# Half-row h.h score matmuls for two heads at once, and context products two slot blocks at a time

## The chip, the cores and the metric

The kernel runs on one core of a Trainium2 chip. Its engines are TensorE (PE: matmuls, with PEld for the loading of the stationary operand), VectorE (DVE), ScalarE (ACT), GpSimd (POOL) and SyncE (SP, which issues DMAs). The metric is the device time of one execution in microseconds (us). Three executions were timed: median 1238.76 us, from 1238.45 to 1245.84. The execution that the profiler recorded took 1251.64 us.

## The reference

Self-attention over 16 batches of 1024 tokens with width 512, with 8 heads of 64, in which the queries are keys and values too, added to the input:

```
q      = x^T Wq^T                     # per batch: 1024 x 512, seen as 8 heads of 64
scores = 0.125 * q q^T                # per head
logits = (scores * cmask + (1 - cmask) * -1e30) * rmask
ctx    = softmax(logits) q
out    = x + (ctx Wo^T)^T
```

The mask is 0 or 1 with about even odds. A masked row has equal logits, so its context is the mean of all q. An unmasked row needs only the unmasked tokens. The kernel therefore gathers the unmasked tokens of a batch into at most 544 slots and computes the attention among these.

## The kernel before, in words

**Precision.** q is split into two f16 parts, q = h + l. The scores of a head need h.h + h.l + l.h. `qsplit` (L388) makes a tile `hl` for each pair of heads (head 0 of the pair in rows 0 to 63, head 1 in rows 64 to 127; h first, l second), and copies it by six DMAs into a tile `xx`, in which each head has all 128 rows, once as h over l and once as l over h. For head k of the pair, xx[:, 2k] is the first and xx[:, 2k+1] the second.

**Scores.** `scores` (L497) makes, for one head and one block of 128 slots (i = 0 to 3), a 128 x 544 tile in PSUM, in two halves of 272 columns (g), each in a bank of its own. The stationary operand is h over l. Two matmuls over all 128 rows add up in each half: with h over l again (h.h + l.l) and with l over h (h.l + l.h). That makes four matmuls for each head and block (L530), 2048 in all. Then ScalarE takes the exponential into an SBUF tile `p` (L533), with the row sums. The score buffers (`pss`) are two, of two banks each. The tail of 32 slots (512 to 543) of four heads at a time is made in `scores(b, p, None)` (L510 to L524), in columns of 32.

**Context.** `attend` (L538) multiplies `p` of the two heads of a pair with the values, in f32: per block two halves of columns for each of two heads, four products (L546), each writing 64 of the 128 PSUM rows (head 0 the lower, head 1 the upper). The tail (i = 4, L549) closes the sum, and ScalarE copies the only context buffer `pav` out (L553).

**Order.** `run` (L724) goes batch by batch over 18 steps S: for each of four pairs the blocks 0 to 3, and two tail steps put in at places 2 and 11. In each step it issues the scores of both heads, and fills with a share of a list m: transposes (`xt`), queries (`query`, L380), values and the rest of the next batch, and the projection of the last one (L625). The share goes by the costs that stand in the list. `todo` holds the context products of the last block (the `attend` of one step is issued in the next), before or after the fill as `big` says. `whole` and `tail` carry the closing product of a pair into the next pair's first steps, between its two heads' scores. `free` holds, by step, work without a place in the list: `recip` two steps after a pair ends and `norm` four. What the loops issue is then put in order, engine by engine, by the framework's scheduler, which has costs of its own and follows the dependencies and the buffers; TensorE runs that order as it stands.

Of the kernel before, what the change touches and what calls it, by code (L numbers as in the profile page):

```python
# [10 lines left out]
F32 = mybir.dt.float32  # L11
F32R = mybir.dt.float32r
F16 = mybir.dt.float16
I32 = mybir.dt.int32
AF = mybir.ActivationFunctionType
# [4 lines left out]
P = 128  # L20
# [3 lines left out]
DK = 64  # L24
# [3 lines left out]
SCALE = 0.125  # L28
NEG = -1.0e30

C = 544
CT = C - 512
CH = C // 2
CQ = C + 2
CM = C
HG = H // 2
# [13 lines left out]
class Fast:  # L50
# [242 lines left out]
            s["xt"] = self.rows(s["idx"][:CT, 4:5], self.sb([P, D], F32, "xt"))  # L293

    def start(self, b):
        s = self.st[b] = {"xa": [], "xx": [], "v": [], "c": [], "nm": [], "corr": [], "rd": [], "xm": []}
        s["ms2"] = self.sb([P, 2 * DC], F32, "ms2", 2)

    def load_half(self, b, k, after=None):
# [88 lines left out]
    def qsplit(self, b, e):  # L388


        nc, s = self.nc, self.st[b]
        q = s["q"][:, e, :C]
        hl = self.sb([P, 2, C], F16, "hl", 1)
        nc.vector.tensor_copy(hl[:, 0, :], q)
        nc.vector.tensor_tensor(hl[:, 1, :], q, hl[:, 0, :], ALU.subtract)
        xx = self.sb([P, 4, C], F16, "xx", 5)
        lo, up = slice(0, DK), slice(DK, P)
        nc.sync.dma_start(out=xx[lo, 0:2, :], in_=hl[lo, :, :])
        nc.sync.dma_start(out=xx[up, 0, :], in_=hl[lo, 1, :])
        nc.sync.dma_start(out=xx[up, 1, :], in_=hl[lo, 0, :])  # L400
        nc.sync.dma_start(out=xx[lo, 2:4, :], in_=hl[up, :, :])
        nc.sync.dma_start(out=xx[up, 2, :], in_=hl[up, 1, :])
        nc.sync.dma_start(out=xx[up, 3, :], in_=hl[up, 0, :])
        s["xx"].append(xx)
# [92 lines left out]
    def scores(self, b, p, i):  # L497


        nc, s = self.nc, self.st[b]  # L500
        if "z" not in s:
            s["z"] = self.sb([P, H, 4], F32, "z", 2)
            s["zt"] = self.sb([P, 2], F32, "zt", 2)
        if i is None:
            pt = self.ps_s.tile([P, 2, 512], F32, tag="s", name="pss")
            for a in range(2):
                for g in range(2):
                    for r in range(HG):
                        xx, k = s["xx"][2 * p + r // 2], r % 2
                        nc.tensor.matmul(pt[r * CT:(r + 1) * CT, g, :CH], lhsT=xx[:, 2 * k, 512:C],  # L510
                                         rhs=xx[:, 2 * k + a, g * CH:(g + 1) * CH], start=(a == 0), stop=(a == 1))
            t = self.sb([P, C], F32, "p", 5)
            nc.scalar.activation(t.rearrange("p (g c) -> p g c", g=2), pt[:, :, :CH], AF.Exp,  # L513
                                 bias=s["nm"][p][:, HG:], scale=SCALE, accum_out=s["zt"][:, p:p + 1])

            hi = self.sb([P, C], F32R, "c", 3)
            lo = t.bitcast(F32R)
            nc.vector.tensor_copy(hi, t)
            nc.vector.tensor_tensor(lo, t, hi.bitcast(F32), ALU.subtract)
            s["pt"] = self.sb([P, 2, C], F32R, "pt")  # L520
            half = slice(0, DK), slice(DK, P)
            for k in range(2):
                nc.sync.dma_start(out=s["pt"][half[k], k, :].bitcast(F32), in_=hi[half[k]].bitcast(F32))
                nc.sync.dma_start(out=s["pt"][half[1 - k], k, :].bitcast(F32), in_=lo[half[k]].bitcast(F32))  # L524
            return None
        xx, k = s["xx"][p // 2], p % 2
        pt = self.ps_s.tile([P, 2, 512], F32, tag="s", name="pss")
        for a in range(2):
            for g in range(2):
                nc.tensor.matmul(pt[:, g, :CH], lhsT=xx[:, 2 * k, i * P:(i + 1) * P],  # L530
                                 rhs=xx[:, 2 * k + a, g * CH:(g + 1) * CH], start=(a == 0), stop=(a == 1))
        t = self.sb([P, C], F32, "p", 5)
        self.exp = [nc.scalar.activation(t.rearrange("p (g c) -> p g c", g=2), pt[:, :, :CH], AF.Exp,  # L533
                                         bias=s["nm"][p // HG][:, p % HG:p % HG + 1], scale=SCALE,
                                         accum_out=s["z"][:, p, i:i + 1]).ins]
        return t

    def attend(self, b, p, i, ps):  # L538
        nc, s = self.nc, self.st[b]
# [184 lines left out]
    def run(self, flag):  # L724
        B = self.B
        L = lambda f, *a: lambda: f(*a)
        S = [(p, i) for p in range(NP) for i in range(4)]
        S.insert(2, (0, None))
        S.insert(11, (1, None))
        N = len(S)  # L730

        def xt(n):
# [16 lines left out]
        for i, e in enumerate(ends):  # L749
            g = list(range(ends[i - 1] + 1 if i else 0, e + 1))  # L750
# [50 lines left out]
        begin += [(0, L(self.load, "o", c)) for c in range(DC)]  # L801
        begin += [(0, L(self.range_x, 0, c)) for c in range(DC)] + [(0, L(self.range_w, "q"))]
        groups = [(g, min(h, B)) for g, h in ((2, 4), (4, 8), (8, 12), (12, 16)) if g < B]
        todo, whole, tail = [], [], []
        for b in range(B + 1):
            o, n = b - 1, b + 1
            if b == B:
# [2 lines left out]
            free, early, late = {}, [], []  # L810
# [67 lines left out]
            for st, (p, i) in enumerate(S):  # L878
                for f in free.get(st, []):
                    f()  # L880
                if i is None:
                    self.scores(b, p, None)
                else:
                    ps = [self.scores(b, 2 * p, i)]
                    if tail:
                        tail.pop()()
                    ps.append(self.scores(b, 2 * p + 1, i))
                goal = total * (st + 1) / N
                fill = []
                while pos < len(m) and (done + m[pos][0] / 2 <= goal or st == N - 1):  # L890
                    fill.append(m[pos])
                    done += m[pos][0]
                    pos += 1

                big = st >= 4 and [c >= 1 for c, _ in fill if c > 0.1][:1] == [True]
                fill = [f for _, f in fill]
                now = [] if i is None else todo
                for f in fill + now if big else now + fill:
                    f()
                if i is not None:  # L900
                    todo = [L(self.attend, b, p, i, ps)]
                if whole and i == 0:
                    tail.append(whole.pop())
                if i == 3:
                    (whole if p < 3 else todo).append(L(self.attend, b, p, 4, None))
                    if p < 3:
                        free.setdefault(st + 2, []).append(L(self.recip, b, p))
                        free.setdefault(st + 4, []).append(L(self.norm, b, p))
            self.st.pop(b - 4, None)
        bad = self.const.tile([1, 1], F32, name="bad")  # L910
        self.nc.vector.tensor_reduce(bad, self.ok[0:1, :], AX.X, ALU.add)
# [145 lines left out]
```

## Time and profile before

| | |
|---|---|
| median of three executions | 1238.76 us |
| profiled execution, its own time | 1251.64 us |
| its span | 1249.9 us |
| TensorE matmuls busy | 1140.9 us (91%) |
| VectorE busy | 714.8 us (57%) |
| ScalarE busy | 693.6 us (55%) |
| GpSimd busy | 296.0 us (24%) |
| mean granted TensorE clock | 0.966 |
| context products L546, busy | 328.7 us in 2048 records |
| score matmuls L530, busy | 309.7 us in 2048 records |

In a line of a group stand the source line, the engine, the operation, the tiles written and read, the shapes and the count; then the busy time in us and the mean in ns of one, and the idle time of the engine just before them with what ended most of it. In "128*64 128x272" the first figures are the rows and columns of the array that are in use, the second the moving operand. The ends of matmuls are modelled and overlap with the next starts, so what one costs is read from start to start. In a timeline a row is: start in us, length in us, engine, line, operation, tiles, shape and count of what was merged into it.

### The profile page before, as it was taken

Reading aid. Unit: us, or ns where it says so; the run is one execution under the profiler, and the core shown is the slowest. Engines: PE = TensorE matmul, PEld = TensorE weight load, DVE = VectorE, ACT = ScalarE, POOL = GpSimd, SP = SyncE. Lnnn points to the kernel's source line nnn. Section 1 sums busy time; section 2 is a strip of 40 time slices with the busy share of each in tenths; the row PEclk is TensorE's granted clock in tenths of the full one; section 3 lists DMA queues with packets and bytes.
Section 4 is the critical chain, followed back from the end, with each engine's and each line's share of the span. In section 5 each row is a group of like instructions: output and inputs, shape, how many; then the busy total and the mean of one; then the engine's idle time right before and its main releaser. Section 6 shows DMA issues by size and latency. Waiting matters only on the chain. (4 is left out here: it accounts for less than half of the span.)

```text
span 1249.9 us, 23817 instructions
## 1 busy us (share of the span) xinstructions
PE 1140.9 (91%) x8354; PEld 694.5 (56%) x8354; DVE 714.8 (57%) x2262; ACT 693.6 (55%) x1828; POOL 296.0 (24%) x299
## 2 busy tenths in 40 slices
PE   7889989998998999999898999999989989998787
PEld 6456555555665555556565555555556555655343
DVE  6576556484645648465464746647565564746433
ACT  5757555565665555556564656556456455545341
POOL 3010221222012123221124314121331222122631
PEclk8899999999999999989999999899999989999889
DMA  6645445555345555545456455454645545444631
GB/s 210 166 125 147 141 128 153 157 161 161 89 138 141 167 149 150 159 122 146 134 140 205 133 149 160 126 150 129 205 129 153 140 142 138 110 138 119 211 114 68
DMA packets 106479, 181.36 MB, mean 145 GB/s; under 512 B 28096, under 2 KB 46176, under 8 KB 106352
## 3 DMA queue, kind: packets, MB, share of 16 engines
q1 hardware_dynamic: 85168, 111.59, 33.4%
q0 software_dynamic: 21184, 68.18, 17.1%
q8 instruction: 68, 1.11, 0.4%
q14 instruction: 59, 0.48, 0.1%
HBM read 92.34 MB, written 33.87 MB: 101 GB/s over the span
## 5 line engine op out<-in xcount | busy, mean ns | idle before, releaser
L533 ACT ACTIVATE p<-pss,nm 128x544 f32<-128x544 f32 x512 | 363.8, 714 | 270.2 <-PE pss L530 190.1
L530 PE MATMUL pss<-xx 128*128 128x272 f16 x2048 | 309.7, 284 | 43.9 <-ACT p L533 24.5
L546 PE MATMUL pav<-p,v 128*64 128x272 f32 x2048 | 328.7, 411 | 15.3 <-issue 11.4
L530 PEld LDWEIGHTS <-xx 128*128 128x128 f16 x2048 | 186.1, 99 | 138.6 <-issue 106.2
L694 POOL DMA_INDIRECT y_out<-xa,idx x72 | 76.9, 1068 | 661.0 <-DVE xa L630 633.7
L546 PEld LDWEIGHTS pav<-p,v 128*64 128x64 f32 x2048 | 132.1, 137 | 134.5 <-issue 80.9
L380 PE MATMUL pm<-xh,wqh 128*128 128x274 f16 (+1 forms) x512 | 147.7, 288 | 20.0 <-ACT q L383 19.7
L380 PE MATMUL pm<-xh,wql 128*128 128x274 f16 (+1 forms) x512 | 147.4, 288 | 0.0
L380 PE MATMUL pm<-xl,wqh 128*128 128x274 f16 (+1 forms) x512 | 147.2, 287 | 0.0
L380 PEld LDWEIGHTS <-wqh 128*128 128x128 f16 x1024 | 101.6, 100 | 48.3 <-issue 25.9
L383 ACT ACTIVATE q<-pm 128x272 f32<-128x272 f32 (+1 forms) x128 | 50.9, 398 | 96.8 <-PE pm L380 69.6
L533 ACT ACTIVATION_READ_ACCUMULATOR p<-pss,nm 128x1 f32 x512 | 102.1, 199 | 0.0
L284 POOL DMA_INDIRECT xa<-x_in,idx x72 | 73.1, 1016 | 90.7 <-ACT p L513 52.1
L630 DVE SCALAR_TENSOR_TENSOR xa<-pm,xa 128x512 f32<-128x512 f32 (+1 forms) x61 | 42.1, 689 | 90.5 <-PE pm L625 86.7
L625 PE MATMUL pm<-woh,ch 128*128 128x512 f16 x240 | 92.8, 387 | 0.0
L625 PE MATMUL pm<-wol,ch 128*128 128x512 f16 x240 | 92.4, 385 | 0.0
L625 PE MATMUL pm<-woh,cl 128*128 128x512 f16 x240 | 92.1, 384 | 0.0
L309 ACT ACTIVATE xm<-xm 128x512 f32<-128x512 f32 x116 | 73.0, 630 | 1.6 <-DMA xm<-x_nat_in 1.6
L694 POOL DMA_INDIRECT y_out<-xi,idx x56 | 58.9, 1051 | 62.1 <-DVE r L568 21.7
L625 PEld LDWEIGHTS <-ch 128*128 128x128 f16 x480 | 47.5, 100 | 46.8 <-issue 3.5
L609 DVE TENSOR_TENSOR c<-c,rb 128x544 f32<-128x544 f32 x64 | 46.1, 721 | 43.7 <-DMA rb<-rd 38.6
L319 DVE SCALAR_TENSOR_TENSOR xl<-pm,xh 128x512 f16<-128x512 f32 (+1 forms) x75 | 44.3, 607 | 33.8 <-ACT xh L318 29.3
(194 smaller groups left out, 1550.6 us busy)
## 6 DMA issues: line engine op xcount, KB each, us to landing
xm<-x_nat_in SPq DMA_DIRECT2D x116, 256.0 KB
xx<-hl SPq DMA_DIRECT2D x256, 68.0 KB
xx<-hl SPq DMA_DIRECT2D x128, 136.0 KB
rb<-rd SPq DMA_DIRECT2D x128, 128.0 KB
pt<-c SPq DMA_DIRECT2D x64, 136.0 KB
pt<-p SPq DMA_DIRECT2D x64, 136.0 KB
ub<-ud SPq DMA_DIRECT2D x16, 256.0 KB
xi<-x_nat_in SPq DMA_DIRECT2D x8, 256.0 KB
```

The source lines that it names most:

```text
L284: self.pool = [self.nc.gpsimd.indirect_dma_start(out=tile[:n], out_offset=None, in_=self.x, in_offset=bass.IndirectOffsetOnAxis(ap=idx, ax ...
L309: self.nc.scalar.activation(s["xm"][k], s["xm"][k], AF.Copy, accum_out=s["ms2"][:, k:k + 1])
L319: self.xs = nc.vector.scalar_tensor_tensor(self.xl[dst], src, SX, self.xh[dst], ALU.mult, ALU.subtract).ins
L380: nc.tensor.matmul(pq, lhsT=w[:, c, e * P:(e + 1) * P], rhs=xx[:, c, cols], start=(k == 0), stop=(k == 3 * DC - 1))
L383: nc.scalar.activation(s["q"][:, e, cols], pq, AF.Copy, scale=1.0 / (SX * SW))
L530: nc.tensor.matmul(pt[:, g, :CH], lhsT=xx[:, 2 * k, i * P:(i + 1) * P], rhs=xx[:, 2 * k + a, g * CH:(g + 1) * CH], start=(a == 0), stop=(a ...
L533: self.exp = [nc.scalar.activation(t.rearrange("p (g c) -> p g c", g=2), pt[:, :, :CH], AF.Exp, bias=s["nm"][p // HG][:, p % HG:p % HG + 1 ...
L546: nc.tensor.matmul(s["pav"][k * DK:(k + 1) * DK, g, :CH], lhsT=s["v"][p][:, i, k * DK:(k + 1) * DK], rhs=ps[k][:, cols], start=(i == 0), s ...
L609: nc.vector.tensor_tensor(c, c, s["rb"][p], ALU.mult)
L625: nc.tensor.matmul(po[:cols.stop - cols.start], lhsT=a[:, e, cols], rhs=w[:, e, :], start=(e == 0 and k == 0), stop=(e == DC - 1 and k == 2))
L630: self.nc.vector.scalar_tensor_tensor(x, po, 1.0 / (SX * SW), x, ALU.mult, ALU.add)
L694: i = self.nc.gpsimd.indirect_dma_start(out=self.out, out_offset=bass.IndirectOffsetOnAxis(ap=idx, axis=0), in_=x, in_offset=None).ins
```

## The change

It has two parts.

`scores` now makes a block for both heads of a pair at once. The full-row matmuls with l over h stay (h.l + l.h, two for each head). The full-row matmuls with h over l are gone. In their place h.h comes straight out of `hl`: the lower 64 rows for head 0 and the upper 64 for head 1, four half-row matmuls in turn (g outside, k inside). The l.l term, which the full-row form brought along, is left out. `hl` must live as long as its scores, so it has five buffers in place of one. Both score buffers are taken at the start of the block.

The context products are collected: `todo` of two blocks becomes `ready` at blocks 0 and 2, and is issued at blocks 1 and 3, ahead of the fill. So a block's products come up to three steps after its scores, and `p` has nine buffers in place of five. A pair's closing product is issued ahead of the next pair's scores of block 2. The second tail step moves from place 11 to 13, and `norm` from four to five steps after the pair's end.

```diff
-        hl = self.sb([P, 2, C], F16, "hl", 1)
+        hl = self.sb([P, 2, C], F16, "hl", 5)
+        s["hl"].append(hl)
...
-            t = self.sb([P, C], F32, "p", 5)
+            t = self.sb([P, C], F32, "p", 9)
...
-        xx, k = s["xx"][p // 2], p % 2
-        pt = self.ps_s.tile([P, 2, 512], F32, tag="s", name="pss")
-        for a in range(2):
+        xx, hl = s["xx"][p], s["hl"][p]
+        blk = slice(i * P, (i + 1) * P)
+        pts = [self.ps_s.tile([P, 2, 512], F32, tag="s", name="pss") for _ in range(2)]
+        for k in range(2):
             for g in range(2):
-                nc.tensor.matmul(pt[:, g, :CH], lhsT=xx[:, 2 * k, i * P:(i + 1) * P],
-                                 rhs=xx[:, 2 * k + a, g * CH:(g + 1) * CH], start=(a == 0), stop=(a == 1))
...
+                nc.tensor.matmul(pts[k][:, g, :CH], lhsT=xx[:, 2 * k, blk], rhs=xx[:, 2 * k + 1, g * CH:(g + 1) * CH],
+                                 start=True, stop=False)
+
+        for g in range(2):
+            for k in range(2):
+                half = slice(k * DK, (k + 1) * DK)
+                nc.tensor.matmul(pts[k][:, g, :CH], lhsT=hl[half, 0, blk], rhs=hl[half, 0, g * CH:(g + 1) * CH],
+                                 start=False, stop=True)
...
-        S.insert(11, (1, None))
+        S.insert(13, (1, None))
...
-                    ps = [self.scores(b, 2 * p, i)]
-                    if tail:
-                        tail.pop()()
-                    ps.append(self.scores(b, 2 * p + 1, i))
+                    if i == 2 and whole:
+                        whole.pop()()
+                    ps = self.scores(b, p, i)
...
-                big = st >= 4 and [c >= 1 for c, _ in fill if c > 0.1][:1] == [True]
                 fill = [f for _, f in fill]
-                now = [] if i is None else todo
-                for f in fill + now if big else now + fill:
+
+                now = []
+                if i in (0, 2):
+                    ready, todo = todo, []
+                elif i in (1, 3):
+                    now, ready = ready, []
+
+                for f in now + fill:
                     f()
                 if i is not None:
-                    todo = [L(self.attend, b, p, i, ps)]
-                if whole and i == 0:
-                    tail.append(whole.pop())
+                    todo.append(L(self.attend, b, p, i, ps))
...
-                        free.setdefault(st + 4, []).append(L(self.norm, b, p))
+                        free.setdefault(st + 5, []).append(L(self.norm, b, p))
```

More of the change, by code (lines that the diff above doesn't have):

```diff
@@ L295, in start @@
     def start(self, b):
-        s = self.st[b] = {"xa": [], "xx": [], "v": [], "c": [], "nm": [], "corr": [], "rd": [], "xm": []}
+        s = self.st[b] = {"xa": [], "xx": [], "hl": [], "v": [], "c": [], "nm": [], "corr": [], "rd": [], "xm": []}
         s["ms2"] = self.sb([P, 2 * DC], F32, "ms2", 2)
@@ L525, in scores @@
             return None
-        xx, k = s["xx"][p // 2], p % 2
-        pt = self.ps_s.tile([P, 2, 512], F32, tag="s", name="pss")
-        for a in range(2):
+        xx, hl = s["xx"][p], s["hl"][p]
+        blk = slice(i * P, (i + 1) * P)
+        pts = [self.ps_s.tile([P, 2, 512], F32, tag="s", name="pss") for _ in range(2)]
+        for k in range(2):
             for g in range(2):
-                nc.tensor.matmul(pt[:, g, :CH], lhsT=xx[:, 2 * k, i * P:(i + 1) * P],
-                                 rhs=xx[:, 2 * k + a, g * CH:(g + 1) * CH], start=(a == 0), stop=(a == 1))
[L532 to L536, printed above, removed]
+                nc.tensor.matmul(pts[k][:, g, :CH], lhsT=xx[:, 2 * k, blk], rhs=xx[:, 2 * k + 1, g * CH:(g + 1) * CH],
[5 more added lines that the diff above has]
+                                 start=False, stop=True)
+        ts = []
+        for k in range(2):
+            h = 2 * p + k
+            t = self.sb([P, C], F32, "p", 9)
+            self.exp = [nc.scalar.activation(t.rearrange("p (g c) -> p g c", g=2), pts[k][:, :, :CH], AF.Exp,
+                                             bias=s["nm"][h // HG][:, h % HG:h % HG + 1], scale=SCALE,
+                                             accum_out=s["z"][:, h, i:i + 1]).ins]
+            ts.append(t)
+        return ts
     def attend(self, b, p, i, ps):
@@ L803, in run @@
         groups = [(g, min(h, B)) for g, h in ((2, 4), (4, 8), (8, 12), (12, 16)) if g < B]
-        todo, whole, tail = [], [], []
+        todo, ready, whole = [], [], []
         for b in range(B + 1):
```

## The prediction

> **What bounds the kernel now.** I read the page first: which engine is busy, then the costliest groups.
>
> ```profile
> PE 1140.9 (91%) x8354; PEld 694.5 (56%) x8354; DVE 714.8 (57%) x2262; ACT 693.6 (55%) x1828; POOL 296.0 (24%) x299
> ...
> L533 ACT ACTIVATE p<-pss,nm 128x544 f32<-128x544 f32 x512 | 363.8, 714 | 270.2 <-PE pss L530 190.1
> L530 PE MATMUL pss<-xx 128*128 128x272 f16 x2048 | 309.7, 284 | 43.9 <-ACT p L533 24.5
> L546 PE MATMUL pav<-p,v 128*64 128x272 f32 x2048 | 328.7, 411 | 15.3 <-issue 11.4
> ```
>
> TensorE (PE) is busy for 91% and no other engine for more than 57%; ScalarE's exponentials (L533) mostly wait for the scores (190.1 us), the scores (L530) for them only 24.5 us. So the kernel is bound by TensorE, and the change edits its two largest groups. Next the waits of TensorE alone, to see what is not TensorE's own work:
>
> ```profile
> PE pss L530 <- ACT p L533: 24.5, 13, 4.4
> PE pm L380 <- ACT q L383: 19.7, 8, 2.9
> PE pav L546 <- issue: 11.4, 6, 4.6
> PE pss L530 <- DMA xx<-hl: 6.8, 2, 4.1
> PE pss L530 <- issue: 6.4, 9, 1.6
> PE pss L530 <- ACT p L513: 5.8, 12, 2.0
> PE pav L546 <- ACT c L553: 3.9, 6, 0.9
> ```
>
> They are few and long, some 90 us in all; the rest of the span is TensorE's instructions in a row. Their durations on the page overlap (284 ns for a matmul that is followed 116 ns later by the next), so I cost them from start to start, in the timeline:
>
> ```profile
> 602.47 0.28 PE L380 MATMUL pm<-xh,wqh 128*128 128x272 f16 x1
> 602.59 0.28 PE L380 MATMUL pm<-xl,wqh 128*128 128x272 f16 x1
> 602.70 0.28 PE L380 MATMUL pm<-xh,wql 128*128 128x272 f16 x1
> 602.91 1.14 PE L546 MATMUL pav<-p,v 128*64 128x272 f32 x8
> 603.98 1.10 PE L530 MATMUL pss<-xx 128*128 128x272 f16 x8
> ```
>
> ```profile
> 337.68 0.41 PE L530 MATMUL pss<-xx 128*128 128x272 f16 x2
> 338.02 0.43 PE L358 MATMUL pm<-ident,xt 32*128 32x32 f32 x4
> 338.38 0.40 PE L530 MATMUL pss<-xx 128*128 128x272 f16 x2
> 338.72 0.67 PE L546 MATMUL pav<-p,v 128*64 128x272 f32 x2
> 339.32 0.27 PE L464 MATMUL pm<-ident,sm 128*4 128x128 f32 x1
> ```
>
> Three prices come out of these.
> (1) A 272-column f16 matmul over all rows costs 0.116 us: L380's pitch, and (1.10 - 0.28) / 7 in the row of eight.
> (2) Changing the array's shape (the figures "128*128", "128*64", "32*128") costs about 0.0935 us each way. The first context product starts 0.21 after the matmul before it, not 0.116. Start by start, the four 32-row transposes at 338.02 come 210 ns after a score matmul, where 116 is its pitch, and the score after them comes 154 ns after the last of them, where 61 is theirs: 94 and 93 ns. So it is charged for shapes with fewer rows as for those with fewer columns.
> (3) An f32 context product is two records, and the products of two heads run side by side (starts 7 ns apart). Four products (eight records) take 1.07 until the next matmul starts, one alone (two records, at 338.72) 0.60. With the shape change that ends both, 1.07 is two slots and 0.60 is one: a slot costs 0.46, and a visit 0.05 besides its two shape changes. One product alone fills a slot as two do.
>
> **What the change does to TensorE's order.** The written loops do not decide it: a scheduler with costs of its own does, and the built program shows its order. In that of before, context products stand in 314 visits with 554 slots (512 would be the least), and the shape changes 751 times. In the changed program I count:
> - 1024 half-row score matmuls, in 373 runs. With A and B for the two heads: ABAB 155 times, AA 128, A 60, ABA 28, AB 2. Where A and B are neighbours they use different rows and, I take it, run side by side. That gives 310 + 256 + 60 + 56 + 2 = 684 slots.
> - 284 visits of context products with 605 slots; 112 visits hold one product. The pairing of two blocks is complete in 45 runs of eight; 29 more have seven.
> - 1269 changes of shape.
>
> The reason is visible in it: where the scheduler held that the second head's buffer is not free yet, it sent one head's full matmuls and its h.h pair, then part of the context, then the other head.
>
> **The sum.**
> - Score matmuls: 1024 - 684 = 340 slots saved, by 0.1156: -39.3 us. As the loop writes it, it would be 512 slots, -59.2.
> - Shape changes: 518 more, by 0.0935: +48.4.
> - Context slots: 51 more, by 0.46: +23.5; 30 visits fewer, by 0.05: -1.5.
> - TensorE's own work: +31.1 us. It lies on the path: TensorE has nothing beside it that could hide it.
> - Waits. The context products of a pair now come steps after the copy (L553) of the buffer they overwrite: the 3.9 us of that wait go. What is late next is TensorE's own queue. On the other side both score buffers are now filled together, so the second head's exponential ends 2 x 0.91 us (714 + 199 ns, L533 and its accumulator read) after the scores; the next scores wait only where less than that lies between. Behind a waiting score stand the query, value and projection matmuls, and through their evictions DVE and ScalarE. In the new order the gaps are mostly over 2 us, but more of them are under it than before. Bounds: -10 us (a third of the 30.3 us that scores wait for exponentials goes, since a slower TensorE gives ScalarE more room) to +15 us (half as much is added); I take 0, as the row of before is small.
> - The rest costs nothing: the same number of exponentials, DMAs and DVE casts. hl in five buffers lets go of the old rule that the next cast waits for the DMAs out of hl (1.9 us, 2 times in the trace); it now waits for the scores, as xx, also five deep, already does. The tail scores two steps later and norm one step later wait in no queue that TensorE needs at once: their readers (context tails, projection) come a batch's part later; were that cover gone, a norm would cost its 0.72 us product once a pair. SP's and POOL's queues keep their transfers.
>
> Together +27.2 us against the profiled execution, whose span is 1249.9 and whose own time is 1251.64. That one lies 1% above the median of 1238.76, so 27.2 x 0.99 = 26.9 is added to the median: **1266 us**.
>
> **Where a rule and a row differ.** No row of before shows a 64-row shape. The Trainium skill, "TensorEngine Tiling (Array Packing)", Key Properties, says that changing the tiling mode drains the array, and gives no figure; the 32-row row gives 0.094. The same page's Theoretical Speedup promises up to 2x for a contraction of 64 or less. By that alone the h.h half of the scores, 1024 x 0.1156 = 118 us, becomes 59 and the kernel 1180. The rows and the counted order make it 79 plus 48 of shape changes. The price per change for this shape lies between 0 and 0.094 us; I take the upper end, because the nearest row (fewer rows, same columns) shows it on both sides.
> A second rule speaks against the trace. "TensorE: Matmul & The Clock Gate", Part 3, has weight loads overlap running matmuls only if the row groups differ; then each score matmul would now cost 0.098 (its load) + 0.116. Its pitch of 0.116 shows the load hidden, so I charge no load to either version beyond the shape change, where it can't be hidden.
>
> **Rivals.**
> - Slower by the order (above), 0.64: 1266, with its waits 1252 to 1284.
> - Faster: the half-row shape changes cheaply. 746 of the changed program's shape changes touch a half-row run. At price 0 the sum is 31.1 - 69.8 = -38.7, with the wait -42.6: 1197. At half price it is about -7.7: 1231. It decides from 0.057 us a change down (27.2 / 746 = 0.036 less than 0.0935). For it: no row of 64 rows. Against: both neighbours of the transposes and the 4-row transposes (211 where 116 is the pitch) pay in full. 0.24.
> - The half-row matmuls do not run side by side. Then 340 slots return: +39, 1304. The 7 ns between column neighbours and the 3 ns of the four tail products (L510) speak against it. 0.05.
> - It does not do what it says, and the array treats 64 rows as its full shape: no pairs, no shape change for them. Left are the context's split slots (+22) and fewer changes (725 in place of 751, -2.4): +19.3, with the wait +15.4: 1254. 0.07.
>
> **How the numbers follow.** 1% (12.4 us) is about what a measurement of this kernel can tell from no change. Slower by over 1%: 0.62 + 0.05 + 0.05 = 0.72. Faster by over 1%: the part of the second case with a price under 0.040, 0.16. Within: 0.12. The range 1220 to 1290 leaves out the cheap end of the second case (0.12), no pairs (0.05) and a little of the first above it.
>
> **What would show it.** In the changed profile: score matmuls of 64 rows ("64*128") in pairs a few ns apart, 0.21 us after the full matmul before them and followed by 0.21 before another shape; lone context products of 0.60; TensorE's busy share at 91% or more with a longer span. A half-row run that starts 0.116 after its predecessor would prove me wrong, as would a fall of the waits for exponentials by more than 10 us.

## The result, and the profile after

The changed kernel took 1246.79 us (median of 20 executions, 1237.07 to 1257.53), the kernel before 1243.46 beside it (20 executions, 1235.4 to 1255.11). The ratio is 1.0039, 95% interval 1.0015 to 1.0062: slower by 0.4%, less than the 1% that the prediction set as the limit of what can be told, and far less than its 2.2%. Some executions fall in a slower state, over 1.5% above the fastest; the ratios, and the differences in us that stand beside them, leave those out, while medians are of all.

In later sets of runs, on two different chips, the ratio was 0.9992 (0.9965 to 1.0019; called the second chip below) and 1.0266 (1.0230 to 1.0301). The chips differ: on some of them the kernel before runs near 1250 us, on others near 1150. Times below are compared within one chip; where two profiles come from different chips, it is said.

First the page of the changed kernel: its engines and its largest groups.

```profile
PE 1163.5 (94%) x8354; PEld 636.1 (51%) x8354; DVE 708.5 (57%) x2262; ACT 692.0 (56%) x1828; POOL 300.6 (24%) x299
...
L544 ACT ACTIVATE p<-pss,nm 128x544 f32<-128x544 f32 x512 | 362.3, 712 | 194.4 <-PE pss L538 154.4
L558 PE MATMUL pav<-p,v 128*64 128x272 f32 x2048 | 342.4, 407 | 1.3 <-issue 1.0
...
L532 PE MATMUL pss<-xx 128*128 128x272 f16 x1024 | 185.5, 284 | 21.1 <-ACT p L544 6.6
...
L538 PE MATMUL pss<-hl 64*128 64x272 f16 x1024 | 145.3, 285 | 0.0
```

The span of this execution is 1236.8 us. TensorE is busy for 1163.5 of it, 22.6 us more than before, and idle for 73.3, where it was 109.0: 35.7 less. So the added work is there, and something gave it back. (These two executions are 13 us apart in favour of the change, while the medians are 3 us apart against it, so part of the 35.7 is the choice of the executions; the second chip's pair, below, is nearer to its medians.) What TensorE still waits for:

```profile
PE pm L586 <- DVE r L584: 21.1, 14, 2.0
PE pss L532 <- ACT p L544: 6.6, 15, 1.1
PE pm L474 <- DVE m L467: 6.2, 1, 6.2
PE pss L532 <- ACT p L514: 5.4, 9, 1.7
PE pss L532 <- issue: 4.6, 6, 1.2
PE pss L532 <- DMA xx<-hl: 3.9, 2, 3.1
```

The long waits for p and q are gone (24.5 to 6.6 us and 19.7 to 1.7, each at most 1.1 us long), and so are the unexplained stops of the context products (11.4 to 1.0). A new wait has come, for the reciprocals r (L584), 21.1 us.

The prices can be read in TensorE's timeline of the changed kernel:

```profile
622.52 0.63 PE L532 MATMUL pss<-xx 128*128 128x272 f16 x4
623.08 0.41 PE L538 MATMUL pss<-hl 64*128 64x272 f16 x4
623.41 0.66 PE L358 MATMUL pm<-ident,xa 128*128 128x128 f32 x4
624.00 0.67 PE L558 MATMUL pav<-p,v 128*64 128x272 f32 x2
624.60 0.41 PE L532 MATMUL pss<-xx 128*128 128x272 f16 x2
624.94 0.29 PE L538 MATMUL pss<-hl 64*128 64x272 f16 x1
625.21 0.66 PE L358 MATMUL pm<-ident,xa 128*128 128x128 f32 x4
625.80 0.29 PE L538 MATMUL pss<-hl 64*128 64x272 f16 x1
626.02 0.67 PE L558 MATMUL pav<-p,v 128*64 128x272 f32 x2
```

At 623.08 four half-row products take 0.33 us until the next shape starts: two slots and a shape change. From 624.00 on it goes wrong: one context product alone (0.60), one head's full matmuls and half-row products, torn apart by a transpose, then again one context product. Start by start over the whole trace, a half-row run begins 212 ns after the full matmul before it (337 times), another shape begins 206 ns after its last product, and a half-row product of the other head follows at 3 ns 340 times, the number counted before. Two of the same head follow at 124 ns.

### The profile page after: what moved, and what is told of

The parts are those of the page before. It is cut to its first block, busy times and chain, and to the rows that moved or that the text cites. A ratio compares the mean times of both kernels' runs of the same rounds, so it can differ in the third digit from the quotient of the medians.

```text
span 1236.8 us, 23535 instructions
## 1 busy us (share of the span) xinstructions
PE 1163.5 (94%) x8354; PEld 636.1 (51%) x8354; DVE 708.5 (57%) x2262; ACT 692.0 (56%) x1828; POOL 300.6 (24%) x299
## 5 line engine op out<-in xcount | busy, mean ns | idle before, releaser
L558 PE MATMUL pav<-p,v 128*64 128x272 f32 x2048 | 342.4, 407 | 1.3 <-issue 1.0
L558 PEld LDWEIGHTS pav<-p,v 128*64 128x64 f32 x2048 | 147.7, 137 | 113.3 <-issue 49.4
L532 PE MATMUL pss<-xx 128*128 128x272 f16 x1024 | 185.5, 284 | 21.1 <-ACT p L544 6.6
L538 PE MATMUL pss<-hl 64*128 64x272 f16 x1024 | 145.3, 285 | 0.0
L380 PE MATMUL pm<-xh,wql 128*128 128x274 f16 (+1 forms) x512 | 143.1, 280 | 0.0
L532 PEld LDWEIGHTS <-xx 128*128 128x128 f16 x1024 | 83.2, 98 | 103.1 <-issue 74.5
L383 ACT ACTIVATE q<-pm 128x272 f32<-128x272 f32 (+1 forms) x128 | 50.8, 397 | 125.1 <-PE pm L380 100.8
L380 PEld LDWEIGHTS <-wqh 128*128 128x128 f16 x1024 | 93.7, 97 | 44.8 <-issue 28.4
L565 ACT COPY c<-pav 128x544 f32<-128x544 f32 x64 | 39.2, 613 | 88.8 <-PE pav L561 74.9
L538 PEld LDWEIGHTS <-hl 64*128 64x128 f16 x1024 | 40.7, 94 | 82.8 <-issue 81.4
L706 POOL DMA_INDIRECT y_out<-xi,idx x56 | 63.4, 1132 | 72.0 <-DVE xi L702 38.0
```

The lines of the kernel that those rows point to most:

```text
L380: nc.tensor.matmul(pq, lhsT=w[:, c, e * P:(e + 1) * P], rhs=xx[:, c, cols], start=(k == 0), stop=(k == 3 * DC - 1))
L383: nc.scalar.activation(s["q"][:, e, cols], pq, AF.Copy, scale=1.0 / (SX * SW))
L532: nc.tensor.matmul(pts[k][:, g, :CH], lhsT=xx[:, 2 * k, blk], rhs=xx[:, 2 * k + 1, g * CH:(g + 1) * CH], start=True, stop=False)
L538: nc.tensor.matmul(pts[k][:, g, :CH], lhsT=hl[half, 0, blk], rhs=hl[half, 0, g * CH:(g + 1) * CH], start=False, stop=True)
L558: nc.tensor.matmul(s["pav"][k * DK:(k + 1) * DK, g, :CH], lhsT=s["v"][p][:, i, k * DK:(k + 1) * DK], rhs=ps[k][:, cols], start=(i == 0), s ...
L565: nc.scalar.copy(c.rearrange("p (g c) -> p g c", g=2), s["pav"][:, :, :CH])
```

## The experiments

Three theories of what gave the work back. **A**: the context products come two blocks late, so TensorE has work in hand that does not depend on ScalarE's newest result. **B**: any work added to TensorE is hidden, as ScalarE gets more room. **C**: taking both score buffers at once does it.

### One part at a time, and added work alone

Half-row scores alone, in the kernel before: the new body of `scores`, both heads in a call, the context products as they were.

```diff
-                    ps = [self.scores(b, 2 * p, i)]
                     if tail:
                         tail.pop()()
-                    ps.append(self.scores(b, 2 * p + 1, i))
+                    ps = self.scores(b, p, i)
```

> The half-row scores alone, with the context products in the order of before. By the prices of the prediction and the order of this built program, TensorE's own work is that of before (+0.9 us: 323 score slots saved by the count of its runs, 505 more changes of shape). Theory A, the waits fell because the context products come two blocks late: they are not late here, so waits stay and the time is that of before, within 6 us. Theory B, the waits fell because TensorE has more work of its own and ScalarE so more room: the work is the same here, so again within 6 us. Theory C, the waits fell because both score buffers are taken at once: then they fall here too, and the time is 20 to 30 us under before.

Measured: 1258.49 against 1255.67, ratio 1.0057 (1.0021 to 1.0094), +7 us, a little over the 6 that were expected.

The context part alone: the changed kernel with full-row scores.

```diff
+        for h in (2 * p, 2 * p + 1):
+            xx, k = s["xx"][h // 2], h % 2
...
+            for a in range(2):
+                for g in range(2):
+                    nc.tensor.matmul(pt[:, g, :CH], lhsT=xx[:, 2 * k, i * P:(i + 1) * P],
+                                     rhs=xx[:, 2 * k + a, g * CH:(g + 1) * CH], start=(a == 0), stop=(a == 1))
```

> The context products of two blocks in a row alone, with the later tail and norm, and the scores all full-row, head by head, as before. TensorE's own work by the prices and the order of this program: -3.0 us (641 changes of shape for 751, 577 context slots for 554, 241 visits for 314). Theory A (late context products take the waits away): 25 to 30 us under before. Theory B (more TensorE work hides the waits): within 6 us of before. Theory C (both score buffers at once): within 6 us of before.

Measured, like the next two beside the same 1255.67 of before: 1225.45, ratio 0.9723 (0.9680 to 0.9765), -35 us.

Work added to the kernel before:

```diff
+        if k == 0:
+            nc.tensor.matmul(pt[:, 0, :CH], lhsT=xx[:, 0, i * P:(i + 1) * P], rhs=xx[:, 0, :CH], start=True, stop=True)
         for a in range(2):
```

> The kernel before with one full-row 272-column matmul more for each pair and block, into a buffer that the next one overwrites: 256 more by 0.116 us, and what its order changes, TensorE work +28 us. Theory B (waits make room for added TensorE work): at most 8 us over before. Theory A and C: 25 to 31 us over before, since nothing else changed.

Measured: 1282.93, ratio 1.0191 (1.0144 to 1.0238), +24 us.

And the changed kernel with its half-row products kept together:

```diff
+        with self.behind(full):     # full: the last full-row matmul of the second head
             for g in range(2):
                 for k in range(2):
```

> The changed kernel with one constraint on the order: the four half-row products of a block are queued behind the full-row matmuls of both heads. By the order of this program 239 of the runs are then whole (155 before that), changes of shape fall from 1269 to 1150, TensorE's own work by 31.8 us against the changed kernel. If the order is what the change pays for: 20 to 32 us under the changed kernel, some 17 to 29 us under before. If the waits give it back: within 8 us of the changed kernel.

Measured: 1227.04, ratio 0.9768 (0.9720 to 0.9815), -29 us.

What follows: B falls (24 us of the 28 added show, 27 by the medians), C falls (both buffers at once without the late context products gains nothing), and A is left: the context part alone, whose order was counted at -3 us of work, changes the time by -35 (-30 by the medians). It is a part of several pieces (lateness, pairs of blocks, p nine deep, the later tail and norm), which this run does not tell apart. The changed kernel did not run in this set, so what the order of the half-row products is worth is read from the next one.

### The same on other chips

> The kernel before, for a second profile. Its time has stood near 1250 us in two sets of runs and at 1151 us in a third. If a chip with long pauses of ScalarE is what makes the difference: near 1250 with some 50 us of ScalarE's idle time put down to no engine, or near 1151 with none of it and TensorE's waits under 60 us in all.

> The changed kernel on the same chip as the second profile of before. If the waits that gave back the work were TensorE's waits for a paused ScalarE: on a chip without the pauses the +31 us of TensorE work and the new wait for the reciprocals (21 us) both show, 30 to 55 us over before; on a chip with the pauses within 8 us of before, as the first time. If the waits fell for another reason: within 8 us of before on either chip.

> The changed kernel with the half-row products behind both heads' full-row matmuls, as before, on this chip. TensorE work equal to that of before (+0.2 us), waits for the reciprocals as in the changed kernel. Without pauses of ScalarE: 10 to 30 us over before, some 20 to 32 under the changed kernel. With pauses: 20 to 32 us under both, as the first time.

> The context part alone on this chip. TensorE work -3 us against before, waits for the reciprocals added (14.8 us the first time). Without pauses of ScalarE: 5 to 20 us over before. With pauses: 25 to 35 us under before, as the first time.

Measured on the second chip: before 1255.36, changed kernel 1253.57 (ratio 0.9992, 0.9965 to 1.0019), with half-row products together 1230.24 (0.9790, 0.9745 to 0.9835), context part alone 1223.95 (0.9755, 0.9677 to 0.9833). The second profile of before took 1254.75. Keeping the half-row products together is worth 23.3 us here against the changed kernel (by the medians), where the count of its order said 31.8.

These profiles show the mechanism. ScalarE in the kernel before (its first profile):

```profile
304.40 0.62 ACT L309 ACTIVATE xm<-xm 128x512 f32<-128x512 f32 x1
304.92 0.19 ACT L309 ACTIVATION_READ_ACCUMULATOR xm<-xm 128x1 f32 x1
308.79 0.40 ACT L383 ACTIVATE q<-pm 128x272 f32<-128x272 f32 x1 [3.68 <-remote]
309.09 0.40 ACT L447 CAST vt<-tmp 128x256 fp32r<-128x256 f32 x1
```

and TensorE at the same time:

```profile
304.01 0.28 PE L380 MATMUL pm<-xh,wql 128*128 128x272 f16 x1
304.22 1.14 PE L546 MATMUL pav<-p,v 128*64 128x272 f32 x8
305.29 1.10 PE L530 MATMUL pss<-xx 128*128 128x272 f16 x8
309.24 0.28 PE L380 MATMUL pm<-xh,wqh 128*128 128x274 f16 x1 [2.85 <-ACT q L383]
```

ScalarE stops for 3.68 us in front of the eviction L383, whose operand (the query matmul at 304.01) is long done. "remote" means that a semaphore (a counter that one engine raises and another waits for) ended the wait, but that no instruction which raises it ends in the profile shortly before. The trace's record of that semaphore says more. It is the one by which TensorE reports finished matmuls. The matmuls that end by the profile at 304.29, 305.93 and 306.39 have no report until 308.77, and then three within 0.2 us; ScalarE goes on at 308.79. So ScalarE does not rest of its own: word of TensorE's work reaches it late, in a bunch. All the "remote" waits of ScalarE, on every chip that has them, are for this semaphore.

TensorE has just finished its context products and filled both score buffers. The next query needs a buffer that L383 must free, so TensorE stops as well. Such a stop costs more than its own length. After another one, 300 us later, the query matmuls start 0.23 us apart in place of 0.12 until 610.6, with a granted clock of 0.50:

```profile
607.94 0.39 PE L380 MATMUL pm<-xh,wqh 128*128 128x274 f16 x1 [2.86 <-ACT q L383]
608.12 0.43 PE L380 MATMUL pm<-xl,wqh 128*128 128x274 f16 x1
608.35 0.43 PE L380 MATMUL pm<-xh,wql 128*128 128x274 f16 x1
...
610.84 0.28 PE L380 MATMUL pm<-xl,wqh 128*128 128x272 f16 x1
610.96 0.28 PE L380 MATMUL pm<-xh,wql 128*128 128x272 f16 x1
```

This trace has 18 stretches with that clock, 3.4 to 10.2 us long and 88.2 us in sum; the 15 of them away from the two ends began when TensorE had stood still for 1.7 to 2.8 of the 3.4 us before. The trace of the changed kernel has 11, 51.8 us in sum.

Now the changed kernel on the second chip, ScalarE:

```profile
310.05 0.19 ACT L309 ACTIVATION_READ_ACCUMULATOR xm<-xm 128x1 f32 x1
313.76 0.40 ACT L383 ACTIVATE q<-pm 128x272 f32<-128x272 f32 x1 [3.51 <-remote]
```

and TensorE:

```profile
309.26 0.62 PE L558 MATMUL pav<-p,v 128*64 128x272 f32 x2
309.81 0.29 PE L380 MATMUL pm<-xh,wqh 128*128 128x272 f16 x1
...
311.10 0.28 PE L380 MATMUL pm<-xh,wql 128*128 128x272 f16 x1
311.31 0.65 PE L511 MATMUL pss<-xx 128*32 128x272 f16 x16
311.89 0.29 PE L380 MATMUL pm<-xh,wqh 128*128 128x274 f16 x1
...
313.06 0.28 PE L380 MATMUL pm<-xl,wqh 128*128 128x274 f16 x1
313.70 0.28 PE L380 MATMUL pm<-xh,wql 128*128 128x274 f16 x1 [0.36 <-issue]
```

The same pause in front of the same line, and TensorE works through it but for 0.36 us. The pauses themselves remain: on the second chip 53.8 us of ScalarE's idle time are "remote" before p, q and c in the kernel before, and 45.8 in the changed one. TensorE stood still during 32.5 us of the first and 14.7 of the second. Its idle time falls from 113.6 to 82.8 us (spans 1253.0 and 1251.5, busy 1139.4 and 1168.7). In the first pair the "remote" sum fell too, from 59.0 to 24.1 us. The context part alone had even more pauses on the second chip:

```profile
ACT q L383 <- remote: 34.2, 9, 3.8
...
ACT p L535 <- remote: 19.4, 11, 3.8
...
ACT c L556 <- remote: 4.8, 1, 4.8
...
ACT p L513 <- remote: 3.8, 1, 3.8
```

With 2.7 us in front of another line that makes 64.9 us against 53.8 in the kernel before; TensorE stood still during 22.8 of them, and the kernel is faster by 31 us. So it is not that the pauses went; more of them were covered.

### Lateness, pairing, order

Context products two blocks late, but one block at a time (the edit as it differs from the context part alone):

```diff
-                if i in (0, 2):
-                    ready, todo = todo, []
-                elif i in (1, 3):
-                    now, ready = ready, []
+                if i is not None and len(todo) > 1:
+                    now = todo.pop(0)
```

> The kernel before with the context products two blocks later, but one block at a time, not two in a row (p nine deep, the closing product, the tail and norm as in the changed kernel; scores as before). TensorE's own work by its order: +1.0 us (763 changes of shape, 309 visits). If the lateness takes the waits away: 22 to 30 us under before. If it is the pairing of two blocks: within 6 us of before.

Reciprocals later in the changed kernel:

```diff
-                        free.setdefault(st + 2, []).append(L(self.recip, b, p))
+                        free.setdefault(st + 4, []).append(L(self.recip, b, p))
```

> The changed kernel with the reciprocals two steps later (four steps after a pair ends, in place of two). Its order differs by -9.8 us of TensorE work. If the new wait of the transposes for the reciprocals (21.1 us in the profile of the changed kernel) is on the path and the two steps cover it: 25 to 31 us under the changed kernel, some 20 to 27 under before. If another wait takes its place: 10 us under the changed kernel, as the order says, or less.

A fixed order, in the context part alone and in the changed kernel (the latter with the constraint on the half-row products too). `sc` is the last score matmul, `av` the last context product:

```diff
+                    with self.behind(*self.sc):
+                        for f in now:
+                            f()
+                    with self.behind(*self.av):
+                        ps = self.scores(b, p, i)
```

> The context part alone, with a constraint on the order: the scores of a block are queued behind the context products of that step, and these behind the scores of the last one. TensorE work -29.9 us against before (536 changes of shape, 547 slots, 191 visits), -26.9 against the context part alone. If the waits that fell there stay low: 55 to 65 us under before.

> The changed kernel with both constraints on the order (half-row products behind both heads' full-row matmuls; scores behind the context products and these behind the last scores). TensorE work -45.9 us against before, -77.9 against the changed kernel: 250 whole runs, 540 context slots in 172 visits, 1007 changes of shape. If order is what was missing and the waits stay as low as in the changed kernel: 65 to 80 us under the changed kernel, 60 to 75 under before. If a fixed order brings waits for the score buffers back: 30 to 45 under before.

Measured, on a chip where before runs at 1151.05: late 1166.04 (ratio 1.0131, 1.0103 to 1.0158), reciprocals later 1188.53 (1.0318, 1.0282 to 1.0354), fixed order in the context part 1166.12 (1.0124, 1.0088 to 1.0160), fixed order in the changed kernel 1196.88 (1.0397, 1.0368 to 1.0427). Nothing gained: in none of these four profiles does ScalarE have a single "remote" pause, so there was nothing to cover. A second set was meant to tell lateness from pairing, and to see the changed kernel beside these:

> Context products two blocks later, one block at a time; TensorE work +1.0 us. On a chip with ScalarE's pauses (before near 1250): 22 to 30 us under before if the lateness hides the pauses, within 6 us if it is the pairing that does. On a chip without (before near 1150): 10 to 20 us over before, as the first time.

> The context part alone with the order fixed (scores behind the context products, these behind the last scores) and the reciprocals one step later; scores full-row. TensorE work -32.7 us against before. On a chip with pauses, waits as in the context part alone (some 28 us under before): 50 to 65 us under before. On a chip without: the waits for the reciprocals, 30 us in the first form of this order, should fall by half or more, so within 12 us of before, either side.

> The changed kernel with both constraints on the order, on a chip that may have pauses: TensorE work -45.9 us against before, but the waits for reciprocals and score buffers of its first profile (40 us and 18 us) stay. With pauses: 20 to 45 us under before. Without: some 45 us over, as the first time.

> The changed kernel beside these. With pauses within 8 us of before, as twice; without pauses 30 to 55 us over before.

The fixed order in the context part now has the reciprocals at three steps in place of two. This set too fell on a chip without pauses: before 1152.12, late 1165.01 (1.0116, 1.0086 to 1.0146), fixed order in the context part 1164.43 (1.0092, 1.0069 to 1.0116), in the changed kernel 1198.10 (1.0385, 1.0353 to 1.0416), changed kernel 1183.08 (1.0266, 1.0230 to 1.0301). So did the last two runs, on yet another:

> The kernel before, one look. On a chip where it runs near 1150: no pauses of ScalarE in the profile, TensorE's waits near 50 us in place of 100. On one near 1250: as in its other profiles.

> Context products two blocks later, one block at a time. On a chip where before runs near 1250: 22 to 30 us under before if the lateness hides ScalarE's pauses, within 6 us if it is the pairing. Near 1150: 10 to 20 us over before, as twice.

Before 1151.39 in its one run with a profile kept and 1148.98 in the seven beside late, late 1164.72 (ratio 1.0134, 1.0105 to 1.0162). This gave the profile of before without pauses. TensorE there,

```profile
PE 1108.1 (96%) x8354; PEld 684.3 (60%) x8354; DVE 713.8 (62%) x2262; ACT 690.9 (60%) x1828; POOL 294.3 (26%) x299
```

and in the changed kernel without pauses (another chip, where before ran at 1152.12):

```profile
PE 1148.2 (97%) x8354; PEld 631.0 (53%) x8354; DVE 708.3 (60%) x2262; ACT 693.5 (59%) x1828; POOL 299.1 (25%) x299
```

The spans are 1149.7 and 1181.8: 40.1 us more busy, 8.0 less idle (41.6 and 33.6), together +32.1. With no pauses to cover, most of the added work shows.

The three pairs of profiles can be split alike. What the half clock cost is half of the time that TensorE was busy under it; the work at full clock is its busy time less that cost. Before and after, in us:

| | idle | cost of the half clock | work at full clock | span |
|---|---|---|---|---|
| first pair | 109.0, 73.3 | 35.7, 19.5 | 1105.2, 1144.0 | -13.1 |
| second chip | 113.6, 82.8 | 33.3, 26.1 | 1106.1, 1142.6 | -1.5 |
| no pauses (two chips) | 41.6, 33.6 | 8.8, 9.0 | 1099.4, 1139.2 | +32.1 |

So the change adds 36 to 40 us of work wherever it runs. Where there are pauses, 31 to 36 us less idle time and 7 to 16 us less half clock pay for it.

Three expectations failed here. The fixed order in the context part was to run 55 to 65 us under before and ran 14 over (its second form 11, as was then expected). The fixed order in the changed kernel was to save 45.9 us of TensorE's work and is 46 us slower. On the page it is busy for 1100.5 us, 7.6 less than before in its profile without pauses (of another chip), and idle for 96.7 of its 1197.2, 55.1 more. Its work at full clock is 28 us less, but the half clock costs it 29.1 in place of 8.8. Its waits:

```profile
PE pm L588 <- DVE r L584: 26.0, 7, 4.5
PE pm L358 <- DVE tmp L444: 9.5, 5, 2.6
PE pm L176 <- DVE tmp L174: 7.4, 4, 3.2
PE pss L511 <- ACT p L545: 6.1, 12, 0.9
PE pss L532 <- ACT p L545: 6.0, 17, 0.8
PE pss L532 <- ACT p L514: 5.2, 8, 1.4
```

TensorE waits at the short products that VectorE must feed, and at the score buffers; that the forced order lets it do nothing else meanwhile is the likely reason, not tested. The third was that later reciprocals would gain. They took the wait for r away (1.0 us is left), but on a chip where it was only 5.5 us in the changed kernel; 8.0 us of waits of the same transpose for another VectorE operation (L319) came in its place.

## Why the prediction was wrong

**The prices: right.** The half-row shape change costs what the 32-row transposes showed (212 and 206 ns from start to start, which is 96 and 90 over the pitch of 116; the prediction took 94 and 93). The rival of a cheap change is out, as is that of no pairs (3 ns, 340 times) and that of no half-row shape at all.

**The counted order: right in direction, too small, and lucky in its sum.** +31.1 us of TensorE work were counted, and 36 to 40 were added. Without pauses the spans differ by +32.1 and the ratio 1.0266 is +30.6 us, close to the forecast of +27.2; but that is 40 us of work less 8 us of idle time, two errors of opposite sign (9 us too little work, 4 us too little saved in waits). From start to start, waits left out, the score matmuls with their shape changes take 24.8 us more there (251.6 and 276.4), the context products with their tails 19.3 more, and the rest 4 less. The context is near its count (+23.5 and -1.5, with the shape changes of 30 visits fewer); most of what is missing lies with the scores, in small pieces: two products of the same head follow at 124 ns where 116 was charged, and the trace has 533 more shape changes where 518 were counted. The other counts erred the same way: the context part alone, counted at -3 us, has 8 us more work at full clock on the second chip. What one order saves against another fits better: with the half-row products together, work falls by 30.8 us there, of 31.8 counted.

**The waits: this step failed.** The prediction took -3.9 us (the wait for the copy L553) and let all else stand at 0, with -10 us as the bound of the gain. On the second chip TensorE's idle time fell by 30.8 us, and the half clock that follows its stops cost 7.2 less, a term that the prediction did not have; in the first pair's two profiles 35.7 and 16.2. The prediction's own sign for this came: the waits for the exponentials p fell by 17.9 us there, where it had named 10. The bound was built on the 30.3 us that scores wait for exponentials, a third of it, in the belief that ScalarE needed room. ScalarE's own list of waits, in the same profile of before, told otherwise:

```profile
ACT p L533 <- remote: 29.0, 12, 5.3
...
ACT q L383 <- remote: 18.2, 6, 3.7
...
ACT c L553 <- remote: 7.9, 2, 5.0
```

An exponential takes 0.71 us and ScalarE is busy for 55%, so waits of TensorE of 2.9 to 4.6 us, in front of three different lines (for p, for q, and "issue"), are not a queue of ScalarE's work: they go with these pauses. How long TensorE stops then depends on how much ready work the order holds, and the context part adds such work. All of the TensorE waits of that kind, 24.5 + 19.7 + 11.4 us, should have stood as the bound of the gain in waits: -55.6 in place of -10, which with +31.1 gives a case of -24 us beside that of +27. (TensorE's waits are 99.8 us in all, not some 90; and the fourth rival's sum should read +19.6. Neither changes the argument.)

**The new wait for r** (21.1 us) was not seen. The prediction said that the later tail scores wait in no queue that TensorE needs at once. By the code they do: r of the third pair needs the sums of the second tail step, which moved from four steps ahead of that r to one, and its transpose stands in TensorE's queue among the next scores. It was in the profiles of the changed kernel on chips with pauses (21.1 and 19.1 us); without pauses it was 5.5 us, and the kernel before had 10.6 us of waits for r there.

**Left open.** Why the word from TensorE comes late is not shown. The pauses come in front of the same instructions on two chips and last about the same, no instruction packet of the DMA queues lands at the end of most of them, and three other chips have none. On the chips with pauses the trace also lacks some of these reports (1216 in before, where 1295 are due, and 1295 of 1295 without pauses), so that the recording itself has a part in it is not ruled out; and since the ends of matmuls are modelled, neither is that TensorE was late and not only its word. Which piece of the context part covers the pauses is open as well: the run that tells lateness from pairing fell on chips without pauses three times, and the nine buffers of p alone were never tried. The context part alone and the kept-together half-row products were not run on such a chip. So no version is shown to beat both kernels everywhere: where there are pauses, the context part alone is 2.4 to 2.8% faster than before, and where there are none, the kernel before is faster than all that was run beside it.

## What to carry to other kernels

Price a change on TensorE in the order in which the built program really stands: here a pairing that saves 59 us as written saved 39 and paid 70 in shape changes and torn pairs, by a count that was still 5 to 9 us short. Split the waits of the bounding engine into many short ones (a rate) and few long ones (another engine that is held up). Here the second kind was bought back by independent work in the queue, so its whole sum, and the slow clock after each long stop, belong in the bound of what a reordering can gain. When a total comes out right, check its terms too. Before explaining 0.4%, measure the same pair of kernels on a second and third chip.

## What the runs showed of the hardware

- Changing TensorE's shape to 64 rows costs the same 0.09 us each way as to 32 rows (96 and 90 ns over the pitch of 116, against 94 and 93), and two 64-row products of different rows start 3 ns apart.
- The same program ran at 1239 to 1256 us on some chips and at 1149 to 1152 on others. In the slower ones ScalarE stood still for up to 6.6 us at a time until TensorE's reports came, 59.0 us in sum in the first profile of before; in the faster ones there was no such wait.
- In the first profile of before TensorE had a granted clock of 0.50 for 88.2 us, in stretches that began, the ends of the run aside, after it had stood still for 1.7 to 2.8 of the last 3.4 us; in the profile of before without pauses for 27.2 us. The mean granted clock was 0.966 and 0.989. Of the 100 us between these two profiles (of two chips), 67 are TensorE's idle time, 27 the half clock, and 6 the rest.
